# Two chained cross-attention layers: scores ahead of maxima in the fuller slots, V placed by ScalarE's queue, all splits of the prologue on GpSimd

## The chip, the core and the metric

The kernel runs on one core of one Trainium2 chip. The metric is the device time of one execution in microseconds (us). Before the change three runs took 943.01, 943.53 and 947.35 us; the median is 943.53 us.

The engines are named as in the profile: PE is TensorE's matrix multiplication and PEld its loading of weights, DVE is VectorE, ACT ScalarE, POOL GpSimd, and SP is SyncE, which here only issues DMAs. SPq and ACTq are the instruction queues of SP and ACT where they issue DMAs.

## What is computed

Two cross-attention layers follow one another over 32 sequences of 256 rows and 320 channels, with 20 heads of 16 channels, and 77 rows of context (512 channels). Cut to what matters, with the reference's other branches (which see no rows here) left out:

```python
for layer in (0, 1):                       # x: (32, 256, 320), ctx: (32, 77, 512)
    q = heads(x @ Wq)                      # 20 heads of 16 channels
    k, v = heads(ctx @ Wk), heads(ctx @ Wv)
    p = softmax(q @ k.T / sqrt(16))        # 256 x 77 for each head
    x = merge(p @ v) @ Wo + b + x
```

All of it is float32.

## The kernel before, in words

**Units.** Two sequences in one layer make a unit; there are 32 units. `units_in_order` (L86) takes the first layer four pairs ahead of the second, so that consecutive units do not depend on each other. Channels lie on partitions; a unit's 20 heads are five groups g of four tiles j, each tile two heads.

**Steps of a unit.** `keys` and `keys_rest` (L318, L336) project the context (`psk`), ACT copies it out (`kR`), and `mask_keys` writes two masked copies `kT`, on POOL but for the first unit (L274). `queries` and, for most units, `outputs_and_queries` (L358, L388) project x (`psq`), and ACT copies to `q`. `split_queries` (L297) divides q into a high and a low part that add up to it (`halves`, two buffers, three pieces of columns: L278 casts, L279 subtracts); `spread_queries` (L307) has SP issue four DMAs for each piece that lay the parts out anew (`qs`). `split_keys` and `spread_keys` do this to the keys (`kS`).

`maxima` (L491) multiplies q by kT (`psm`, L500) into four PSUM banks, and DVE takes maxima over the keys (`m`, L512). When all of a unit's are there, `turn` (L522) has DVE split and transpose them (L532 to L535, some 1.7 us) and SP issue four DMAs (L537) to `max_rows`. `scores` (L545) computes scores less maxima (`pss`: L550 with `max_rows`, L558 with `qs` and `kS`) into four PSUM banks, and ACT takes exponentials (`pT`, L564). `vals` (L428; `vals_of_few` for the last, short chunk) projects V for a chunk of 128 context rows (`psv`), ACT copies it to a `stage` (L442), and `place_vals` (L466) has a queue issue DMAs that put the rows of one unit into its tile `v`, mostly three for a unit (L485), and four more for the short chunk of each layer (L480). `values` (L607) multiplies pT by v (`po`, L578); DVE transposes (L590) and takes reciprocals (L594), POOL multiplies (L599), `turn_back` (L610) transposes once more on DVE to `oT` (L613). `finish` or `outputs_and_queries` projects it (`psy`), and `add` (L616) adds bias and x on DVE.

**Banks.** All products share eight PSUM banks that go round (`bank`, L108). A product begins when the bank that it takes has been read by the engine that empties it. In a slot with maxima and scores, the product behind them, the first `po`, takes the first bank of the eight: that of whichever of the two came first.

**Slots.** The order of the work is written out by hand. `at` (L656) puts a step under a slot number and a kind; L799 goes through the slots and emits the kinds of each in one fixed order: load, maxima, turn back, scores, values, rest, back, turn, split, full, last. Each engine runs its own instructions in this order. Slots below 1 are the prologue (L760 to L787). In steady state four units take 17 slots. The text names four kinds:

- A full slot (F) holds `outputs_and_queries`, mostly two `scores` and no `maxima`.
- Slot A behind it holds maxima, one `scores`, two `values`, `keys_rest`, the first half of a chunk's `vals`, `place_vals` of the older chunk, and in about half of the units `turn`.
- Slot B holds maxima, one `scores`, one `values`, one `keys`, the second half of `vals` and `place_vals` of the new chunk.
- Slot C holds maxima, one `scores`, one `values` and one `keys`.

Every DMA also waits for the completion of one that was issued about eight DMAs before it, on whichever queue that one is.

Of the kernel before, what the change touches and what calls it, by code (L numbers as in the profile page):

```python
# [58 lines left out]
B, S, C, CA, L = 32, 256, 320, 512, 77  # L59
# [36 lines left out]
def xattn_kernel(ctx: ExitStack, tc: tile.TileContext, xT, cT, cP, weights, outT):  # L96
    nc = tc.nc
# [46 lines left out]
    first, _, _ = PARTS["q"]  # L144
# [152 lines left out]
    def split_queries(u, i):  # L297

        a, b = PIECES[i]
        x = st[u]["halves", i] = work.tile(  # L300
            [P, 2, NT], F32R, tag="halves", name=f"halves_{u}_{i}", bufs=2
        )
        split(
            nc.gpsimd if u else nc.vector, x[:, 0, : b - a], x[:, 1, : b - a], st[u]["q"][:, a:b]
        )

    def spread_queries(u, i):  # L307
# [10 lines left out]
    def keys(u, t):  # L318
        p, layer = units[u]
        w, c_sb = w_sb[layer], cs[u]  # L320
        if t == 0:
            st[u]["kr"] = work.tile([P, NG, L], F32, tag="kR", name=f"kR_{u}", bufs=2)
        kR = st[u]["kr"]
        ps = bank(f"psk_{u}_{t}")
        for kc in range(NKA):
            by_columns(
                ps[:, 0 : 2 * L],
                w["k"][:, kc, t * P : (t + 1) * P],
                c_sb[:, kc, :],
                start=(kc == 0),  # L330
                stop=(kc == NKA - 1),
            )
        nc.scalar.copy(kR[:, 2 * t : 2 * t + 2].rearrange("p g k -> p (g k)"), ps[:, 0 : 2 * L])  # L333
        mask_keys(u, t)

    def keys_rest(u):  # L336

        p, layer = units[u]
        w, c_sb = w_sb[layer], cs[u]
        ps = bank(f"psk_{u}_2")  # L340
        for kc in range(NKA):
            for i in range(4):
                b, m = 1 - i // 2, i % 2
                nc.tensor.matmul(  # L344
                    ps[32 * i : 32 * i + 32, 0:L],
                    w["k"][:, kc, 2 * P + 32 * m : 2 * P + 32 * m + 32],
                    c_sb[:, kc, b * L : (b + 1) * L],
                    start=(kc == 0),
                    stop=(kc == NKA - 1),
                )  # L350
        nc.scalar.copy(st[u]["kr"][:, 4], ps[:, 0:L])
        mask_keys(u, 2)
# [5 lines left out]
    def queries(u):  # L358

        p, layer = units[u]  # L360
        w = w_sb[layer]
        q0 = new_queries(u)
        ps = [[bank(f"psq_{u}_{t}_{b}") for b in range(NB)] for t in range(2)]
        if u == 0:

            main_channels(ps, w["q"], xs[p], start=True, stop=False)
            last_channels(ps, w["q2"], xs[p], start=False, stop=True)
        else:
            rest = bank(f"psq_{u}_2")
            last_channels(ps, w["q2"], xs[p], start=True, stop=False)  # L370
            for b in range(NB):
                rest_last(rest, w["q22"], xs[p], b, swap=1, start=True, stop=False)
            rest_main(rest, w["q"], xs[p], start=False, stop=True, swap=1)
            nc.scalar.copy(of_group(q0, 4), rest[:, 0:S])
            main_channels(ps, w["q"], xs[p], start=False, stop=True)
        for g in range(4):
            nc.scalar.copy(of_group(q0, g), ps[g // 2][g % 2][:, 0:S])
# [88 lines left out]
    def place_vals(u, i):  # L466

        p, layer = units[u]
        if "v" not in st[u]:
            st[u]["v"] = work.tile(  # L470
                [P, NB, HEADS // 2, 2, 2, HD], F32, tag="v", name=f"v_{u}", bufs=2
            )
        for b in range(NB):
            first = (p * NB + b) * L
            k0, k1 = max(first, i * P), min(first + L, (i + 1) * P)
            if k0 < k1 and i in few:

                for m, a, r0, r1 in ((0, 0, 0, 3), (1, 0, 3, 6), (2, 0, 6, 9), (3, 2, 9, 10)):
                    o = 32 * m - i * P
                    nc.sync.dma_start(  # L480
                        out=st[u]["v"][k0 - first : k1 - first, b, r0:r1],
                        in_=stages[layer][i % 2][k0 + o : k1 + o, a : a + r1 - r0],
                    )
            elif k0 < k1:
                nc.sync.dma_start(  # L485
                    out=st[u]["v"][k0 - first : k1 - first, b],
                    in_=stages[layer][i % 2][k0 - i * P : k1 - i * P],
                )
# [118 lines left out]
    def values(u, g):  # L607
        st[u]["n", g] = divide(u, g, products(u, g))
# [44 lines left out]

    place = {}

    def at(slot, where, step):  # L656
        place.setdefault((slot, where), []).append(step)

    def start(u):

# [18 lines left out]
    for u, (p, layer) in enumerate(units):  # L679

        s = start(u - 2)
        if layer == 0 and u > 0:
            at(s - 5 - (u == 1), "load", lambda p=p: load_x(p))
        if u > 0:
            at(s - 4, "load", lambda u=u: load_context(u))
        if u > 1:
            k = (0, 1, 2) if u == 2 else (s - 2, s - 1, s + 1)
            at(k[0], "rest", lambda u=u: keys(u, 0))
            at(k[1], "rest", lambda u=u: keys(u, 1))
            at(k[2], "rest", lambda u=u: keys_rest(u))  # L690
        paired = u > 2 and u - 3 not in late
        if paired:
            at(s, "full", lambda u=u: outputs_and_queries(u - 3, u))
        elif u > 1:
            at(s, "last", lambda u=u: queries(u))
        if u > 1:
            at(s + 2, "split", lambda u=u: split_keys(u))
            at(start(u - 1), "load", lambda u=u: spread_keys(u))
            for i in range(3):
                at(start(u - 1) + i - 1, "split", lambda u=u, i=i: split_queries(u, i))  # L700
                at(start(u - 1) + i, "load", lambda u=u, i=i: spread_queries(u, i))
        need = range(p * NB * L // P, ((p + 1) * NB * L - 1) // P + 1)
        new = [i for i in need if i >= made[layer]]
        made[layer] += len(new)
        first = (-6, -2)[u] if u < 2 else start(u - 1) + 1
        slots = {}
        for k, i in enumerate(new):
            at(first - 3 - (u == 0) + k, "load", lambda layer=layer, i=i: load_chunk(layer, i))
            if i in few:
                slots[i] = first  # L710
                at(first, "full", lambda layer=layer, i=i: vals_of_few(layer, i))
                continue
            for h in range(2):
                slots[i] = first + (0 if u < 2 else k if len(new) > 1 else h)
                at(slots[i], "full", lambda layer=layer, i=i, h=h: vals(layer, i, h))
        for i in need:
            at(slots.get(i, first), "full", lambda u=u, i=i: place_vals(u, i))
        for g in range(NG):
            slot = slot_of(u, g)
            at(slot, "scores", lambda u=u, g=g: scores(u, g))  # L720
            at(slot + 1, "values", lambda u=u, g=g: values(u, g))
            if g < 4:
                at(slot + 2, "turn back", lambda u=u, g=g: turn_back(u, g))
            else:
                at(slot + 1, "back", lambda u=u, g=g: turn_back(u, g))
        if u == NU - 1:
            at(end, "full", lambda u=u: finish(u))
            at(end, "last", lambda u=u: finish_rest(u))
        if u in late:
            for t in range(2):  # L730
                at(late[u][t], "full", lambda u=u, t=t: finish(u, (t,)))
            at(late[u][2], "rest", lambda u=u: finish_rest(u))
            at(max(late[u]), "last", lambda u=u: store(u))


# [30 lines left out]
    at(-7, "split", lambda: split_keys(0))  # L766
    at(-6, "load", lambda: spread_keys(0))
    for i in range(3):
        at(-6 + i, "split", lambda i=i: split_queries(0, i))
        at(-5 + i, "load", lambda i=i: spread_queries(0, i))  # L770
    for slot, h, n in ((-6, 0, 3), (-6, 3, 3), (-4, 6, 2), (-4, 8, 2)):
        at(slot, "maxima", lambda h=h, n=n: maxima((0, h, n)))
    at(-4, "turn", lambda: turn(0))
# [1 line left out]
    at(-3, "split", lambda: split_keys(1))  # L775
    at(-2, "load", lambda: spread_keys(1))
    for i in range(3):
        at(-3 + i, "split", lambda i=i: split_queries(1, i))
        at(-2 + i, "load", lambda i=i: spread_queries(1, i))
    for slot, h, n in ((-2, 0, 3), (-2, 3, 2), (0, 5, 3)):  # L780
        at(slot, "maxima", lambda h=h, n=n: maxima((1, h, n)))
    at(1, "maxima", lambda: maxima((1, 8, 2), (2, 0, 1)))
# [2 lines left out]
    for u, slot in ((1, 1), (2, 4)):  # L785
# [7 lines left out]
    at(3, "load", lambda: load_weights(1, "v", "v", nc.sync))  # L793
    at(4, "load", lambda: load_weights(1, "o", "b", nc.sync))

    order = (
        "load", "maxima", "turn back", "scores", "values", "rest", "back", "turn", "split", "full", "last",
    )
    for slot in range(min(s for s, _ in place), max(s for s, _ in place) + 1):  # L799
        for where in order:  # L800
            for step in place.get((slot, where), ()):
                step()
# [98 lines left out]
```

## Time and profile before

| | |
|---|---|
| median of three runs | 943.53 us |
| profiled execution, its own time | 947.08 us |
| span of that execution, first to last instruction | 945.3 us, so 1.8 us lie around it |
| mean granted TensorE clock | 0.998 |
| share of the chain that ended last: PE, DVE, DMA, SPq | 88%, 7%, 2%, 1% |
| PE busy in the first 70 us | 63.0 us |
| PE busy from 60 us on (885.3 us) | 873.5 us |

The profile is one execution, taken by the hardware profiler. A group of instructions shows its busy time, the mean duration of one, the idle time of its engine just before it, and behind an arrow the instruction whose end released it. A row of the timeline starts with its start and its duration in us. Matmuls are pipelined and their ends are modelled, so that a busy PE is not PE at its peak; one float32 matmul appears as two records.

### The profile page before, as it was taken

To read this page: it belongs to the slowest core of one execution; us is meant where nothing else is said; L and a number is where in the kernel's file an instruction comes from. 1 tells how busy PE (TensorE), PEld (TensorE's weight loads), DVE (VectorE), ACT (ScalarE), POOL (GpSimd) and SP (SyncE) were. 2 spreads that over 40 slices of the span, in tenths; PEclk is the share of its full clock that TensorE was granted. 3 is DMA by queue.
4 is the path that set the end of the run, shared out by engine and by line. 5 is a ranking of instruction groups with operands and counts; after the bars stand their busy time and mean duration, and the time that the engine had idled before them with its cause. 6 is when DMAs were issued, how large, how long until landed. Compare 5 with 4: busy or idle time off the path is not lost.

```text
span 945.3 us, 48848 instructions
## 1 busy us (share of the span) xinstructions
PE 926.6 (98%) x21582; PEld 640.8 (68%) x21582; DVE 574.5 (61%) x1330; ACT 432.0 (46%) x975; POOL 406.9 (43%) x608
## 2 busy tenths in 40 slices
PE   8999999999999999999999999999999999999998
PEld 6666667766667666666766677666767666676654
DVE  4475557655577565665656666665566654776575
ACT  2254443644435534355443545335454354444462
POOL 2354445434455434455234454344553335543431
PEclk9999999999999999999999999999999999999999
DMA  6664444253453525536245352355433543353342
GB/s 227 196 217 129 133 147 145 82 172 120 163 153 95 197 76 163 165 104 201 68 145 176 98 201 82 125 175 161 153 96 120 160 155 119 92 162 105 118 136 97
DMA packets 114740, 133.03 MB, mean 141 GB/s; under 512 B 47012, under 2 KB 76004, under 8 KB 114530
## 3 DMA queue, kind: packets, MB, share of 16 engines
q1 hardware_dynamic: 113666, 127.42, 42.8%
q8 instruction: 170, 2.79, 1.3%
q10 hardware_dynamic: 864, 2.49, 0.7%
q14 instruction: 40, 0.33, 0.1%
HBM read 35.39 MB, written 10.49 MB: 49 GB/s over the span
## 4 chain that ended last, share of the span: by engine, by line
PE 88%; DVE 7%; DMA 2%; SPq 1%; issue 1%; POOL 0%; ACT 0%; POOLq 0%
PE psy L203 15%; PE po L578 15%; PE psq L203 14%; PE psm L500 10%; PE psv L203 7%; PE pss L558 7%; PE psk L203 7%; PE psy L237 4%; PE pss L550 4%; PE psq L237 3%; DVE m L512 3%; DVE turned L590 1%; PE psk L344 1%; DVE maxes L533 1%; SPq L316 1%; DMA x<-in_xT_dram 1%
## 5 line engine op out<-in xcount | busy, mean ns | idle before, releaser
L564 ACT ACTIVATE pT<-pss 77x512 f32<-77x512 f32 x640 | 324.4, 593 | 171.7 <-PE pss L558 171.0
L512 DVE TENSOR_REDUCE m<-psm 128x6 f32<-128x462 f32 (+2 forms) x512 | 248.3, 551 | 221.4 <-PE psm L500 220.9
L599 POOL TENSOR_TENSOR normal<-turned,inv 128x256 f32<-128x256 f32 x160 | 99.3, 621 | 484.5 <-DVE inv L594 457.5
L578 PE MATMUL po<-pT,v 77*32 77x256 f32 x2560 | 166.8, 385 | 8.3 <-DVE m L512 5.2
L203 PE MATMUL psy<-oT,w 128*32 128x256 f32 (+1 forms) x3072 | 164.5, 379 | 0.0
L203 PE MATMUL psq<-x,w 128*32 128x256 f32 (+1 forms) x3072 | 153.4, 380 | 0.6 <-DMA w<-in_w_dram 0.6
L203 PEld LDWEIGHTS psy<-oT,w 128*32 128x32 f32 (+1 forms) x3072 | 88.4, 108 | 63.4 <-issue 15.2
L590 DVE STREAM_TRANSPOSE turned<-po 128x512 f32<-128x512 f32 x160 | 109.5, 684 | 24.4 <-PE po L578 24.3
L203 PEld LDWEIGHTS psq<-x,w 128*32 128x32 f32 (+1 forms) x3072 | 86.8, 109 | 54.9 <-issue 2.2
L274 POOL TENSOR_SCALAR kT<-kR,masks 128x154 f32<-128x154 f32 x186 | 113.3, 619 | 19.2 <-ACT kR L333 19.2
L578 PEld LDWEIGHTS po<-pT,v 77*32 77x32 f32 x2560 | 72.4, 109 | 69.6 <-DVE m L512 26.7
L500 PE MATMUL psm<-kT,q 32*128 32x154 f32 x2560 | 116.2, 306 | 2.3 <-POOL kT L274 2.0
L500 PEld LDWEIGHTS psm<-kT,q 32*128 32x128 f32 x2560 | 90.1, 183 | 35.3 <-issue 25.3
L279 POOL TENSOR_TENSOR halves<-q,halves 128x512 fp32r<-128x512 f32 (+1 forms) x93 | 102.1, 1098 | 7.8
L558 PE MATMUL pss<-qs,kS 32*77 32x256 f32 x2560 | 104.6, 276 | 0.0
L620 DVE SCALAR_TENSOR_TENSOR x<-psy,w,x 128x256 f32<-128x256 f32 x160 | 68.3, 476 | 50.6 <-PE psy L203 49.2
L558 PEld LDWEIGHTS pss<-qs,kS 32*77 32x77 f32 x2560 | 89.2, 141 | 11.3
L613 DVE STREAM_TRANSPOSE oT<-normal 128x256 f32<-128x256 f32 x160 | 67.0, 431 | 45.8 <-POOL normal L599 45.8
L203 PE MATMUL psv<-w,cv 128*32 128x160 f32 x2432 | 93.5, 299 | 0.2 <-DVE m L512 0.2
L418 ACT COPY q<-psq 128x256 f32<-128x256 f32 x28 | 10.4, 372 | 161.8 <-PE psq L237 161.8
L203 PEld LDWEIGHTS psv<-w,cv 128*32 128x32 f32 x2432 | 77.8, 110 | 4.4 <-DVE m L512 0.6
L550 PE MATMUL pss<-max_rows,less 32*77 32x512 f32 x640 | 78.7, 468 | 1.4 <-DMA max_rows<-mT 1.4
(48 smaller groups left out, 725.3 us busy)
## 6 DMA issues: line engine op xcount, KB each, us to landing
qs<-halves SPq DMA_DIRECT2D x256, 128.0 KB
kS<-k_halves SPq DMA_DIRECT2D x128, 192.5 KB
c<-in_cP_dram SPq DMA_DIRECT2D x32, 308.0 KB
cv<-in_cT_dram SPq DMA_DIRECT2D x38, 256.0 KB
out_dram<-x SPq DMA_DIRECT2D x15, 640.0 KB
x<-in_xT_dram SPq DMA_DIRECT2D x14, 640.0 KB
qs<-halves SPq DMA_DIRECT2D x128, 64.0 KB
v<-stage SPq DMA_DIRECT2D x26, 192.5 KB
```

What stands on the lines that cost most here:

```text
L203: nc.tensor.matmul(out[m : m + 32], lhsT[:, m : m + 32], rhs, **flags)
L274: engine.tensor_scalar_mul(kT[:, e], kR[:, groups], masks[:, e : e + 1])
L279: engine.tensor_tensor(low, x, high.bitcast(F32), ALU.subtract)
L500: nc.tensor.matmul(ps[j][:, i * 2 * L : (i + 1) * 2 * L], q[r, c * P : (c + 1) * P], kT[r, :, g % 2, :], start=True, stop=True,)
L512: nc.vector.tensor_reduce(st[u]["m"].rearrange("p e h j -> p h e j")[:, first : first + n, :, j], ps[j][:, at * 2 * L : (at + n) * 2 * L]. ...
L550: nc.tensor.matmul(ps[j][:L], less[r, g % 4, :], max_rows[u % 2][r, g // 4], start=True, stop=False)
L558: nc.tensor.matmul(ps[j][:L, e * S : (e + 1) * S], st[u]["ks"][r, e, g, half, :], q[r, :], start=False, stop=(half == 1 and e == 1),)
L564: nc.scalar.activation(st[u]["p", g][j][:L], ps[j][:L], AF.Exp, scale=SCALE)
L578: nc.tensor.matmul(po[o : o + 32, e * S : (e + 1) * S], vpad[:L, b, pair, e].rearrange("p a d -> p (a d)"), pT[j][:L, e * S : (e + 1) * S] ...
L590: nc.vector.transpose(turned[:, 0 : 2 * S], po)
L599: nc.gpsimd.tensor_tensor(normal.rearrange("p q e d -> p e q d"), outs, inv.unsqueeze(3).broadcast_to([P, 2, S // 32, HD]), ALU.mult,)
L620: nc.vector.scalar_tensor_tensor(x, ps[:, 0:S], w_sb[layer]["b"][:, 0, t : t + 1], x, ALU.add, ALU.add)
```

## The change

There are three edits.

1. Steps under `at` carry a count of PE columns (`work_of`). In a slot above 0 whose count is over 10 * S = 2560, the kinds are emitted as load, scores, turn back, maxima; in all other slots as before. By these counts all slots F, A and B come under the new order (A has 3944, 5224 or 4200, B 3536 to 4816), while C (2256), slots of 2304 and the prologue keep the old one. 60 slots have both scores and maxima and the new order.
2. `place_vals` issues its DMAs from ACT's queue instead of SP's: 100 at L485 and 8 at L480.
3. In the prologue `split_queries` of unit 0 goes from DVE to POOL, and the splits and their `spread_queries` stand in earlier slots: pieces 0 and 1 together, right behind the queries, piece 2 one slot later. For unit 1, pieces 0 and 1 come together too, and piece 2 goes to slot 0, behind that slot's `keys`. `split_keys` of unit 0 stays on DVE.

```diff
@@ split_queries
-            nc.gpsimd if u else nc.vector, x[:, 0, : b - a], x[:, 1, : b - a], st[u]["q"][:, a:b]
+            nc.gpsimd, x[:, 0, : b - a], x[:, 1, : b - a], st[u]["q"][:, a:b]
@@ place_vals, in both places
-                nc.sync.dma_start(
+                nc.scalar.dma_start(
@@ at
-    def at(slot, where, step):
+    work_of = {}
+
+    def at(slot, where, step, columns=0):
+
         place.setdefault((slot, where), []).append(step)
+        work_of[slot] = work_of.get(slot, 0) + columns
...
-            at(k[0], "rest", lambda u=u: keys(u, 0))
+            at(k[0], "rest", lambda u=u: keys(u, 0), 8 * 2 * L)
...
-            at(s, "full", lambda u=u: outputs_and_queries(u - 3, u))
+            at(s, "full", lambda u=u: outputs_and_queries(u - 3, u), 50 * S)
...
-                at(slots[i], "full", lambda layer=layer, i=i, h=h: vals(layer, i, h))
+                at(slots[i], "full", lambda layer=layer, i=i, h=h: vals(layer, i, h), 4 * C)
...
-            at(slot + 1, "values", lambda u=u, g=g: values(u, g))
+            at(slot + 1, "values", lambda u=u, g=g: values(u, g), 4 * S)
...
@@ the prologue, unit 0 and unit 1
-        at(-6 + i, "split", lambda i=i: split_queries(0, i))
-        at(-5 + i, "load", lambda i=i: spread_queries(0, i))
+        at(-7 + i // 2, "split", lambda i=i: split_queries(0, i))
+        at(-6 + i // 2, "load", lambda i=i: spread_queries(0, i))
...
-        at(-3 + i, "split", lambda i=i: split_queries(1, i))
-        at(-2 + i, "load", lambda i=i: spread_queries(1, i))
+        at(-3 + 3 * (i // 2), "split", lambda i=i: split_queries(1, i))
+        at(-2 + 3 * (i // 2), "load", lambda i=i: spread_queries(1, i))
@@ the loop over the slots
-    order = (
-        "load", "maxima", "turn back", "scores", "values", "rest", "back", "turn", "split", "full", "last",
-    )
+    rest = ("values", "rest", "back", "turn", "split", "full", "last")
     for slot in range(min(s for s, _ in place), max(s for s, _ in place) + 1):
+        if slot > 0 and work_of[slot] > 10 * S:
+            order = ("load", "scores", "turn back", "maxima") + rest
+        else:
+            order = ("load", "maxima", "turn back", "scores") + rest
```

## The prediction

> **What bounds the kernel.** I read the page first, then the waits by engine, then the timeline: the first 60 us, and one stretch of steady state (226 to 242 us).
>
> ```profile
> PE 926.6 (98%) x21582; PEld 640.8 (68%) x21582; DVE 574.5 (61%) x1330; ACT 432.0 (46%) x975; POOL 406.9 (43%) x608
> L578 PE MATMUL po<-pT,v 77*32 77x256 f32 x2560 | 166.8, 385 | 8.3 <-DVE m L512 5.2
> ```
>
> PE is the bound, and no edit takes a product away. A gain can only come from PE's pauses, 18.7 us in all. The waits say whose they are (total, times, longest):
>
> ```profile
> PEld po L578 <- DVE m L512: 26.7, 89, 1.1
> PE po L578 <- DVE m L512: 5.2, 11, 0.9
> PE psm L500 <- POOL kT L274: 2.0, 1, 2.0
> PE pss L550 <- DMA max_rows<-mT: 1.4, 1, 1.4
> ```
>
> The 26.7 us of PEld are no prize: 89 waits of 0.3 each, and in slot F, where no maxima stand, po's weights also wait 0.28 (at 186.24, named ACT pT). That is the end of the product before. What can be had is 5.2 us in 11 places, and the prologue.
>
> **The prologue.**
>
> ```profile
> 29.05 4.62 SPq L316 DMA_DIRECT2D qs<-halves  x4
> ...
> 34.41 2.71 SPq L537 DMA_DIRECT2D max_rows<-mT  x4
> ...
> 39.95 0.46 PE L550 MATMUL pss<-max_rows,less 32*77 32x512 f32 x4 [1.44 <-DMA max_rows<-mT]
> ...
> 48.17 0.40 POOL L278 CAST halves<-q 128x256 fp32r<-128x256 f32 x1 [4.70 <-DMA qs<-halves]
> ...
> 49.35 1.34 POOL L274 TENSOR_SCALAR kT<-kR,masks 128x154 f32<-128x154 f32 x2
> 50.75 0.55 PE L500 MATMUL psm<-kT,q 32*128 32x154 f32 x8 [2.05 <-POOL kT L274]
> ...
> 52.33 1.94 PE L578 MATMUL po<-pT,v 77*32 77x256 f32 x16
> ```
>
> Two queues are held by pieces of q. SP: mT is ready at 27.95, but its DMAs stand behind those of q's pieces and go out only at 34.41. POOL: unit 2's kT stands behind unit 1's third piece, which waits 4.70 for a buffer; PE then waits 2.05 and comes back at a lower clock (granted 0.50 in 52 to 54 us).
>
> After the change, step by step:
> - Unit 0's splits leave DVE (0.42 + 0.69 twice). Its second reduces start 0.5 earlier, and `psk` at 24.00, which waits for one of them, gains 0.5.
> - POOL splits pieces 0 and 1 (0.61 + 1.28 each, from the steady rows) by about 15 us. SP sends kS at 15.26 to 18.97, then eight qs (0.6 each) to 23.8, two loads, the third piece to 27.4, two loads, and mT at 28.6 instead of 34.41; it lands near 34. L550 then waits only for PE: 2.3 earlier in all.
> - `kT` of unit 2 stands ahead of the third split of unit 1, so the 2.05 goes: 2.3 + 2.05 and the split first part of psm make 4.6 at the second L550.
> - With no pause the clock stays: po costs 0.88 instead of 1.71 to its successor, psk 1.17 instead of 1.53. 6.1 by slot 2.
> - What is late next: DVE. Its 2.54 of reduces, 0.95 of L590 and L594 and 1.7 of `turn` now end 1.3 after PE wants po of slot 2; before, that wait was 0.25. 1.1 comes back.
>
> Sum: **5.0** gained (from 2.3, if kT's wait only changes its name, to 6.1). Three v DMAs on ACT ahead of the first exponentials hold these by about 1; `psq` wants their banks later than that.
>
> **Scores ahead of maxima.**
>
> ```profile
> 231.65 0.29 ACT L442 COPY stage<-psv 128x160 f32<-128x160 f32 x1 [0.86 <-PE psv L203]
> ...
> 232.71 0.45 DVE L535 STREAM_TRANSPOSE mT<-maxes 128x256 f32<-128x256 f32 x1
> ...
> 233.08 2.24 DVE L512 TENSOR_REDUCE m<-psm 128x6 f32<-128x462 f32 x4
> ...
> 233.38 2.04 ACT L564 ACTIVATE pT<-pss 77x512 f32<-77x512 f32 x4 [1.44 <-PE pss L558]
> ...
> 233.74 1.07 PE L578 MATMUL po<-pT,v 77*32 77x256 f32 x16 [0.45 <-DVE m L512]
> ```
>
> This is slot B behind an A with `turn`. The turn keeps DVE to 233.16, the reduce starts late, and po waits 0.45 for its first bank. In the new order po takes the bank of the first exponential: L550 to exponential takes 1.1 (232.31 to 233.38), the exponential 0.59, in all 1.69; L550 to po takes 1.79 (0.72 of scores, 0.84 and 0.25 of maxima, as now in the other order). Slack 0.1. Of the eleven waits nine of 0.44 to 0.46 stand in such slots: **4.1** gained. (The 0.25 of 57.61 is in the prologue, and the 0.90 of 810.68 in a slot that keeps the old order.)
>
> Late next is DVE in slot C. Maxima now end 0.71 later in A, and DVE has no pause from there: 233.08 + 0.71, two L613 (0.67), four reduces (2.16), L590 and L594 (0.96), first reduce of C (0.63) end at 238.21, where C's po wants its bank at 238.66 - 0.45 = 238.21. A knife edge: between 0 and 0.45 each, I take 0.1: **-0.9** (0 to -4.1).
>
> The trace shows no pss ahead of psm and no psm ahead of po. Changes of weights beside them cost 0.16 (psm to psv, 17.68) to 0.42 (35.05); psv to psm 0.25, psv to pss 0.24, pss to po 0.26. Nearest is 0.26, so the 60 slots change by nothing; 0.1 either way would be 6.
>
> **V from ACT's queue.** SP loses 108 issues, but nothing on PE waits for SP in steady state: gain 0. ACT gets them in order, between `stage` copy and the next exponentials.
>
> ```profile
> L120 SPq DMA_DIRECT2D x<-in_xT_dram x14: 347/587/621, 24.2 to 740.8; - x14
> L120 ACTq DMA_DIRECT2D x<-in_xT_dram x1: 334/334/334, 4.8 to 4.8; - x1
> L485 SPq DMA_DIRECT2D v<-stage x100: 593/807/1647, 20.5 to 917.8; - x100
> ```
>
> (Durations: shortest/median/longest.) ACT shows none of this form. One x load took 334 ns on ACT and 587 on SP; v took 807 on SP. Bounds are 0.33 and 0.81; I take 807 x 334/587 = 0.46. An ACT instruction behind a DMA waits for its issue: the table load starts at 7.37, the DMA of 7.00 took 0.34.
>
> B's exponential is due 1.1 after L550, with 0.1 of slack; ACT can issue from 0.13 after L550 (old chunk) or 0.43 (fresh). Slots A with one DMA lose nothing. Seven with two of the old chunk free ACT at 0.13 + 0.92: nothing. One with two fresh ones: 0.15. Six with three, at 0.13 + 1.38 against 1.2: 0.31 each, 1.9. Near the end six DMAs, four of them shorter (L480, 588 ns on SP), hold the exponentials of 912.71 by 1.3. Sum **-3.3** (-0.7 at 0.33, -15.8 at 0.81). B's DMAs stand ahead of C's exponentials, and C's po waits for DVE: nothing, but for a wait on mT's DMAs, which may hold ACT for up to 1.
>
> The Trainium skill, "DMA: Bandwidth & Descriptors" (Issuing engines are not separate DMA queues), says that issuing from several engines saves only sequencer time. It speaks against this edit: SP has that time to spare, ACT pays it. Taken alone it makes the edit a loss.
>
> The skill's "TensorE: Matmul & The Clock Gate" (Part 1) lets the clock fall after an idle window of about 3.4 us. Here a recorded idle of 2.05 went before the 0.50, so the trace differs; by the rule the 1.2 of clock would not return, and the prologue would give an estimated 3.8.
>
> **Sum.** 5.0 + 4.1 - 0.9 - 3.3 = 4.9 off the profiled 947.08: 942.2. That execution was 3.55 above the median of 943.53, so **938.6**.
>
> **Rivals.**
> - *Slower: ACT pays as SP did.* At 0.81 ACT loses 15.8: 5.0 + 4.1 - 0.9 - 15.8 = -7.6, **951.1**. For: L485 never went under 593 on SP. Against: ACT's five early issues took 0.33 to 0.47. It decides from about 0.6 an issue, where ACT eats the 8.2 of the rest.
> - *The wait moves to C:* all 4.1 come back: 1.7, **941.8**. For: DVE's chain has no gap. Against: the arithmetic ends level.
> - *The prologue gives half:* 2.3 instead of 5.0: 2.2, **941.3**. For: SP's queue is in order, and loads stand between the pieces.
> - *All goes well:* ACT at 0.33, no wait in C, 6.1 in the prologue: 6.1 + 4.1 - 0.7 = 9.5, **934.0**.
>
> **Chances.** Forecast 0.30, ACT slow 0.18, wait moves 0.20, prologue halved 0.08, all well 0.24. What a measurement can tell from no change is 0.5%, 4.7 us: 938.8 to 948.2. The forecast lies by its edge; I count 0.18 of it below and 0.12 within. Faster 0.18 + 0.24 = 0.42, same 0.12 + 0.20 + 0.08 = 0.40, slower 0.18. Range 932.5 to 949.5: it takes in the good case with 1.5 for the unseen changes of weights, and the lower half of the slow case, and leaves out about 0.15. The likeliest case alone spans 936 to 941.
>
> **What would show it.** Prologue: the second L550 near 46 instead of 51, no granted clock under 1 at 50 to 55, po of slot 2 waiting over 1 for DVE. Steady state: no `PE po <- DVE m` in B; a new one in C refutes the knife edge; `PE po <- ACT pT` in B behind three DMAs shows ACT's price. I am wrong if L485 on ACT is over 0.6, or if slots in the new order are longer where nothing waits.

## The result and the profile after

The changed kernel takes 991.56 us (median of four runs, 987.96 to 996.11) against 944.53 for the kernel before: ratio 1.0497, 95% interval 1.0446 to 1.0548. The forecast was 938.6, its range 932.5 to 949.5; it was wrong, in sign too.

The profiled execution took 987.96 with a span of 986.2, which is 40.9 more than before. First its line of busy times and the group of po, as the page shows them:

```profile
PE 941.3 (95%) x21582; PEld 642.7 (65%) x21582; DVE 574.5 (58%) x1324; ACT 433.0 (44%) x975; POOL 413.1 (42%) x614
...
L578 PE MATMUL po<-pT,v 77*32 77x256 f32 x2560 | 168.3, 388 | 30.4 <-ACT pT L564 27.4
```

PE does the same 21582 records and is busy 14.7 longer; its idle time goes from 18.7 to 44.9. The wait ahead of po was DVE's; now it is ACT's. The waits by engine (total, times, longest):

```profile
ACT pT L564 <- DMA v<-stage: 45.6, 12, 11.1
...
PE po L578 <- ACT pT L564: 27.4, 16, 8.9
...
PE pss L550 <- DMA max_rows<-mT: 3.4, 2, 2.8
...
PE po L578 <- DVE m L512: 2.5, 2, 1.5
```

The nine waits of 0.45 are gone (the two left are in the prologue and in a slot with the old order). But ACT, for which PE waited nowhere before, now holds its exponentials behind its own V DMAs. By the starts of the 28 F slots:

| stretch | before | after | longer by |
|---|---|---|---|
| start to the first F slot | 69.49 | 72.72 | 3.2 |
| first to 28th F slot | 778.10 | 800.41 | 22.3 |
| 28th F slot to the end | 97.71 | 113.04 | 15.3 |

Two kinds of wait make this up. The first is occupation. The group of L485 and a slot B of the timeline (start, duration):

```profile
L485 ACTq DMA_DIRECT2D v<-stage x100: 553/760/1436, 23.0 to 945.1; - x100
```

```profile
176.94 0.29 ACT L442 COPY stage<-psv 128x160 f32<-128x160 f32 x1 [0.79 <-PE psv L203]
176.95 2.39 ACTq L485 DMA_DIRECT2D v<-stage  x3
...
179.39 2.04 ACT L564 ACTIVATE pT<-pss 77x512 f32<-77x512 f32 x4 [2.15 <-DMA v<-stage]
...
180.03 1.07 PE L578 MATMUL po<-pT,v 77*32 77x256 f32 x16 [1.50 <-ACT pT L564]
```

Three issues of 0.76 in a row keep ACT from the exponentials for 2.15, and po, which in the new order takes the bank of the first of them, waits 1.50. The second kind is a wait inside ACT's queue. The timeline around the A slot at 676:

```profile
669.07 10.96 SPq L316 DMA_DIRECT2D qs<-halves  x8
...
676.13 4.53 ACTq L485 DMA_DIRECT2D v<-stage  x3
...
677.05 0.40 POOL L278 CAST halves<-q 128x256 fp32r<-128x256 f32 x1
...
680.70 2.04 ACT L564 ACTIVATE pT<-pss 77x512 f32<-77x512 f32 x4 [4.36 <-DMA qs<-halves]
...
681.35 1.55 PE L578 MATMUL po<-pT,v 77*32 77x256 f32 x16 [3.72 <-ACT pT L564]
```

Every DMA waits on the semaphore that it raises itself, and eight of these go round both queues. The third V DMA starts at 679.99; the last DMA on its semaphore was one of SP for the third piece of q, which had to wait for POOL's split, went out at 677.47 and landed at 679.97. ACT runs in order, so the exponentials stood behind it. A V DMA that starts within 0.11 us of the landing that it waits for is called held below. In this trace 24 of 108 are held: 12 behind one of mT's (L537), 11 behind a piece of q (L316), one behind V itself. At the end the same happens to all exponentials of one slot:

```profile
942.23 6.06 SPq L316 DMA_DIRECT2D qs<-halves  x8
942.81 3.04 ACTq L485 DMA_DIRECT2D v<-stage  x2
947.10 2.92 ACTq L480 DMA_DIRECT2D v<-stage  x4
950.07 1.56 ACT L564 ACTIVATE pT<-pss 77x512 f32<-77x512 f32 x3 [9.48 <-DMA v<-stage]
950.71 3.64 PE L578 MATMUL po<-pT,v 77*32 77x256 f32 x32 [8.86 <-ACT pT L564]
```

The 32 records of po take 3.64 here and 1.93 at 671.34. The lower clock is where more than half of the 14.7 of busy time come from: the granted clock is 0.50 for 3.4 us beside the pauses at 39, 47, 681 and 835 each, and for 13.7 from 944.6. PE is busy for 21.0 of these 27.3 us, since the last stretch begins inside the long pause; in the kernel before it is 3.4 of 3.4. Half the difference, 8.8, is an estimate of what the clock added.

### The profile page after: what moved, and what is told of

Read it like the earlier page. It is cut to its first block, busy times and chain, and to the rows that moved or that the text cites. A ratio compares the mean times of both kernels' runs of the same rounds, so it can differ in the third digit from the quotient of the medians.

```text
span 986.2 us, 48442 instructions
## 1 busy us (share of the span) xinstructions
PE 941.3 (95%) x21582; PEld 642.7 (65%) x21582; DVE 574.5 (58%) x1324; ACT 433.0 (44%) x975; POOL 413.1 (42%) x614
## 4 chain that ended last, share of the span: by engine, by line
PE 73%; DVE 10%; DMA 4%; issue 4%; POOL 3%; SPq 2%; ACTq 2%; ACT 2%; POOLq 0%; DVEq 0%
PE psq L203 14%; PE psy L203 13%; PE po L578 12%; PE psm L500 6%; PE pss L558 6%; PE psv L203 5%; PE psk L203 5%; DVE m L512 4%; PE pss L550 4%; PE psy L237 4%; PE psq L237 4%; DMA qs<-halves 2%; DVE turned L590 2%; DVE maxes L533 1%; ACTq L485 1%
## 5 line engine op out<-in xcount | busy, mean ns | idle before, releaser
L203 PE MATMUL psq<-x,w 128*32 128x256 f32 (+1 forms) x3072 | 157.3, 382 | 3.8 <-ACT pT L564 3.5
L578 PEld LDWEIGHTS po<-pT,v 77*32 77x32 f32 x2560 | 70.1, 110 | 90.1 <-ACT pT L564 43.4
L500 PE MATMUL psm<-kT,q 32*128 32x154 f32 x2560 | 112.1, 298 | 0.0
L279 POOL TENSOR_TENSOR halves<-q,halves 128x512 fp32r<-128x512 f32 (+1 forms) x96 | 106.8, 1112 | 8.0
L558 PE MATMUL pss<-qs,kS 32*77 32x256 f32 x2560 | 108.0, 276 | 0.0
L500 PEld LDWEIGHTS psm<-kT,q 32*128 32x128 f32 x2560 | 92.6, 184 | 13.8 <-issue 10.2
L550 PE MATMUL pss<-max_rows,less 32*77 32x512 f32 x640 | 85.1, 454 | 5.7 <-DMA max_rows<-mT 3.4
L203 PE MATMUL psk<-c,w 128*32 128x154 f32 x2048 | 81.8, 301 | 0.0
```

Of the source, the lines that this page charges most:

```text
L203: nc.tensor.matmul(out[m : m + 32], lhsT[:, m : m + 32], rhs, **flags)
L279: engine.tensor_tensor(low, x, high.bitcast(F32), ALU.subtract)
L500: nc.tensor.matmul(ps[j][:, i * 2 * L : (i + 1) * 2 * L], q[r, c * P : (c + 1) * P], kT[r, :, g % 2, :], start=True, stop=True,)
L550: nc.tensor.matmul(ps[j][:L], less[r, g % 4, :], max_rows[u % 2][r, g // 4], start=True, stop=False)
L558: nc.tensor.matmul(ps[j][:L, e * S : (e + 1) * S], st[u]["ks"][r, e, g, half, :], q[r, :], start=False, stop=(half == 1 and e == 1),)
L578: nc.tensor.matmul(po[o : o + 32, e * S : (e + 1) * S], vpad[:L, b, pair, e].rearrange("p a d -> p (a d)"), pT[j][:L, e * S : (e + 1) * S] ...
```

## The experiments

**Theory A:** V's DMAs hold ACT, above all by their waits for landings. **B:** the new order itself is slow. **C:** prologue and tail make most of it. **D:** what costs is the time that each issue takes. Differences below are of medians; ratios are to the kernel before, with 95% intervals.

### One edit at a time

Each edit alone on the kernel before, and the changed kernel without the second:

```diff
 v_back_on_sp: the changed kernel, in place_vals
-                nc.scalar.dma_start(
+                nc.sync.dma_start(
 v_on_act_alone: the kernel before, in place_vals
-                nc.sync.dma_start(
+                nc.scalar.dma_start(
 order_alone: the kernel before with work_of and the choice of order
 prologue_alone: the kernel before with split_queries on nc.gpsimd in the new slots
```

> The changed kernel with V's DMAs back on SP's queue: the new order and the new prologue without the second edit. Theory A (ACT is held by V's DMAs: each waits in ACT's queue until a DMA some eight places earlier, most of them SP's, has landed; the exponentials queued behind it come late, and the first po of a slot in the new order takes the bank of the first exponential): the 27.4 us of `PE po <- ACT pT` and the 45.6 of `ACT pT <- DMA v` go, and the time comes to 938 to 944 us. Theory B (the new order itself is slow, ACT's waits are only where it shows): 965 to 990, and the waits of po stay under another name. Theory C (the prologue and the tail make most of it): 955 to 975, F slots level with those of before from the second on.

> The kernel before with the second edit alone: V's DMAs on ACT's queue, old order, old prologue. In the old order the first po takes a bank that DVE empties, and the banks of the scores are wanted only some four products later, so a late exponential has about 2 us more. Theory A: ACT still waits some 30 to 45 us behind V's DMAs, but little of it reaches PE in steady state (0 to 6 us); prologue and tail may pay up to 12: 945 to 960. If it is only the issue time of 0.76 us each, whatever the order: 944 to 950, and no wait of ACT on a DMA above 1 us. If the second edit costs its 48 by itself: 980 to 992.

> The kernel before with the first edit alone: scores ahead of maxima in slots above 2560 columns; V stays on SP, the prologue is the old one. Theory A: the nine waits of 0.45 go, slots C pay 0 to 4: 938 to 944. Theory B (the order is slow): above 955.

> The kernel before with the third edit alone: all splits of the prologue on GpSimd, in earlier slots. By the prediction the second L550 comes near 46 instead of 51 and the time falls by 2.3 to 6.1: 937.5 to 941. By the rival that the prologue itself lost (in the changed kernel the first F slot came 3.2 later): 945 to 948.

| kernel | us | ratio |
|---|---|---|
| v_back_on_sp | 942.98 | 0.9982 (0.9957 to 1.0007) |
| v_on_act_alone | 981.03 | 1.0381 (1.0351 to 1.0412) |
| order_alone | 943.05 | 0.9983 (0.9962 to 1.0003) |
| prologue_alone | 944.71 | 0.9999 (0.9986 to 1.0013) |

B and C fall: without the second edit nothing is lost, and order and prologue alone lose nothing. But A as I had put it falls too. I had expected 945 to 960 for V on ACT in the old order; it took 981.03, 36.0 more than before. Its waits:

```profile
ACT pT L564 <- DMA v<-stage: 47.3, 13, 9.9
...
PE po L578 <- ACT pT L564: 9.3, 1, 9.3
...
PE psq L203 <- ACT pT L564: 6.5, 1, 6.5
```

The slack of some 2 us in the old order hides short waits, and 20 of the 27 steps from F slot to F slot in this trace are within 0.3 of those of before. But seven are 0.9 to 3.7 longer, and prologue and tail take 3.0 and 13.7. The edit is dearer still in the new order: 991.56 - 942.98 = 48.6.

### Occupation without a wait

V stays on SP; where ACT issued its DMAs, it does a copy that waits for no DMA:

```diff
                 nc.sync.dma_start(
                     out=st[u]["v"][k0 - first : k1 - first, b],
...
                 )
+                nc.scalar.copy(junk, ones[:, 0:1].broadcast_to([P, 680]))
```

> The kernel before, with V's DMAs left on SP; in their place ACT does a copy of a constant into an unused tile, 128x680, some 0.7 us long, which waits for no DMA. It puts the occupation of 0.76 us an issue on ACT without any wait behind SP's DMAs, in the old order. Theory A (in the old order the 36 us come from waits for landings, not from the issues): the time stays near that of before, 944 to 948. Theory D (the time that an issue takes is what costs): 970 to 982.

> The same copies on ACT in the kernel that has the first edit alone (943.05 without them). Theory A': in the new order a slot B has little slack behind two or three issues, so the occupation alone shows as `PE po <- ACT pT` of 0.4 to 1.9 in some 14 slots: 954 to 959. If the new order has as much slack as the old one: 943 to 946. Theory D: 970 to 985.

dummy_old_order took 952.52 (1.0075, 1.0051 to 1.0099), dummy_new_order 958.81 (1.0148, 1.0123 to 1.0174). In dummy_new_order (its lines stand 3 lower: L567 and L581 are the exponentials and po) the copy, a slot B and a wait read:

```profile
L491 ACT CAST junk<-ones x100: 757/760/770, 20.5 to 920.2; 128x680 bf16<-128x680 f32 x100
```

```profile
171.45 2.34 ACT L491 CAST junk<-ones 128x680 bf16<-128x680 f32 x3
173.70 2.04 ACT L567 ACTIVATE pT<-pss 77x512 f32<-77x512 f32 x4
...
174.34 1.07 PE L581 MATMUL po<-pT,v 77*32 77x256 f32 x16 [1.48 <-ACT pT L567]
```

```profile
PE po L581 <- ACT pT L567: 18.5, 16, 3.9
```

The copy takes 760 ns, as an issue does, and gives the same wait in the same slot: 1.48 against 1.50. So the occupation costs 958.81 - 943.05 = 15.8 in the new order. In the old one it costs 8.5, more than A expected: the six copies of the last unit hold po for 3.9, and the tail of the profiled execution is 6.9 longer. Of its 27 steps from F slot to F slot only two are over 0.3 longer (0.4 and 1.4). Its prologue is 4.2 shorter than in the profile of before; why, I did not pursue. D falls: of the 48.6, 48.6 - 15.8 = 32.8 are something else than occupation.

### V later on ACT

```diff
-            at(slots.get(i, first), "full", lambda u=u, i=i: place_vals(u, i))
+            at(slots.get(i, first) + 1, "full", lambda u=u, i=i: place_vals(u, i))
```

> The kernel before with V's DMAs on ACT's queue (981.03 as it was), each place_vals one slot later; queue, count and issue time are the same. In the old places those that were held came some three us behind mT's DMAs or the third piece of q on SP. Theory A: a slot later these have landed, so in steady state the steps of 1.5 to 3.7 from F slot to F slot go, and the time falls by 8 to 17, to 964 to 973; prologue and tail may change either way by some 5. Theory D: 978 to 984, no change.

In this kernel a unit that needs two fresh chunks takes the rows of its oldest chunk from the chunk that has overwritten that stage; the amount of work is unchanged. It took 986.33 (1.0426, 1.0377 to 1.0474): no theory's number. Its trace has 17 held DMAs instead of 22: 4 behind mT's instead of 9, but 12 behind pieces of q instead of 10. The wait has moved, not gone. It tells nothing between the theories.

### The held DMAs alone

```diff
+    BACK = {(3, 4), (22, 11), (23, 16), (8, 3), (28, 15), ...}
     def place_vals(u, i):
         p, layer = units[u]
+        queue = nc.sync if (u, i) in BACK else nc.scalar
...
-                nc.scalar.dma_start(
+                queue.dma_start(
```

> The changed kernel (991.56), but the 19 calls of place_vals in which its trace shows a V DMA that started within 0.11 us of the landing that it waits for go back to SP: 34 of 108 DMAs. Theory A (waits for landings cost some 33 of the 48.6 that V on ACT costs in this order, the occupation by 108 issues some 16): the 33 go, and the last unit's occupation with them: 948 to 962, if few others come to be held instead. Theory D (every V DMA on ACT costs alike): 34/108 of 48.6, 15 less: 974 to 979.

> The counterpart: the changed kernel with 34 other V DMAs back on SP, in 24 calls of place_vals none of whose DMAs was held. Theory A: only some of the occupation goes, the waits stay: 983 to 991. Theory D: 974 to 979, as with the other 34.

> The old order and the old prologue with V on ACT (981.03), but the 19 calls of place_vals with held DMAs in that trace on SP, 35 of 108. Theory A: the 73 others cost nothing in the old order: 945 to 952. Theory D: 35/108 of 36.5, 12 less: 967 to 971.

| V on ACT | us | ratio | held |
|---|---|---|---|
| all 108 (changed kernel) | 991.56 | 1.0497 (1.0446 to 1.0548) | 24 |
| without 34, the held ones among them | 958.57 | 1.0145 (1.0112 to 1.0178) | 0 of 74 |
| without 34 others | 986.87 | 1.0434 (1.0405 to 1.0464) | 23 of 74 |
| old order, without 35, the held ones among them | 944.67 | 0.9998 (0.9983 to 1.0013) | 0 of 73 |

This settles it. The same number of DMAs moved is worth 33.0 or 4.7 (the intervals of the changed kernel and of the 34 others overlap). In the old order the 35 make all of the loss, and the other 73 cost nothing on ACT. What is left in held_on_sp is mostly the occupation (its po is L581):

```profile
PE po L581 <- ACT pT L567: 14.9, 15, 1.7
```

The 34 include the six DMAs of the last unit, whose occupation alone held po for 3.9 in dummy_new_order. Of the other waits of po for exponentials, 14.6 there, 14.9 stand here. So the waits for landings cost an estimated 29 of the 33.0.

### Versions that beat both

With V on SP a stall of another kind spreads the runs (937.96 to 948.63). In v_back_on_sp SP sends V behind mT, and ACT's next copy into that stage waits for its landing:

```profile
458.19 3.84 SPq L537 DMA_DIRECT2D max_rows<-mT  x4
...
462.46 2.46 SPq L485 DMA_DIRECT2D v<-stage  x3
...
466.49 0.49 ACT L442 COPY stage<-psv 128x160 f32<-128x160 f32 x2 [5.59 <-DMA v<-stage]
...
466.83 0.90 PE L550 MATMUL pss<-max_rows,less 32*77 32x512 f32 x2 [2.95 <-ACT stage L442]
```

```diff
 v_sp_before_turn: v_back_on_sp with
-            at(slots.get(i, first), "full", lambda u=u, i=i: place_vals(u, i))
+            at(slots.get(i, first), "full" if i in slots else "back", lambda u=u, i=i: place_vals(u, i))
 mt_ahead_of_piece: that, and in the prologue
-        at(-6 + i // 2, "load", lambda i=i: spread_queries(0, i))
+        at(-6 if i < 2 else -4, "load" if i < 2 else "full", lambda i=i: spread_queries(0, i))
```

> The new order and the new prologue with V on SP (942.98, 937.96 to 948.63 in ten runs), but the older chunk's place_vals stands ahead of the slot's turn, so that on SP V's DMAs do not stand behind mT's. In the profile of the version without this, ACT's copy into stage waits 5.6 us for such DMAs in one slot and PE loses 2.9 at 467. If that stall is what spreads the runs: 938 to 941 and a spread of under 4; if mT, now behind V, becomes late instead: 943 to 950.

> The version with V on SP ahead of the turn (940.12), and in the prologue SP issues the third piece of unit 0's q behind mT instead of ahead of it. It tests the step of the prediction that failed in the prologue: mT's DMAs at 28.6, where the run of the third edit alone shows 33.93, behind that piece, and a first L550 that waits 2.67 with a clock of 0.50 behind it. If the piece ahead of mT is what holds mT: mT goes out near 30, the wait of L550 and the slow clock go, and the first F slot comes 3 to 4.5 earlier: 935.5 to 938. If the landing waits of the loads ahead of it hold SP just as long: mT after 32.5, and 939 to 941.

v_sp_before_turn took 940.12 (0.9959, 0.9944 to 0.9975), 939.03 to 943.20: no copy into stage waits for V, and the spread falls from 10.7 to 4.2. mt_ahead_of_piece took 939.10 (0.9938, 0.9921 to 0.9956). Its SP and PE:

```profile
30.70 2.93 SPq L537 DMA_DIRECT2D max_rows<-mT  x4
```

```profile
38.28 0.46 PE L550 MATMUL pss<-max_rows,less 32*77 32x512 f32 x4 [2.44 <-DMA max_rows<-mT]
38.55 0.83 PE L558 MATMUL pss<-qs,kS 32*77 32x256 f32 x16
39.31 2.28 PE L203 MATMUL psk<-c,w 128*32 128x154 f32 x32
```

mT goes out near 30 as hoped, but L550 still waits 2.44 and the slow psk is still there. mT's four DMAs now take 5.1 to 5.8 to land, where they took 2.8 to 4.9 in v_sp_before_turn and 3.3 to 4.3 in the kernel before. From 30 to 34 us the share of the DMA engines reads 1.03, at 326 GB/s; in the kernel before, where mT is in flight from 34 on, it reads 0.80 from 34 to 38, at 200. Loads of cv, x, c and w, 1.7 MB, go out just ahead, from 27.53 on; that they slow the landing is likely, but no run shows it alone. SP sends mT 2.8 earlier than in v_sp_before_turn, and the last of the four lands 0.9 earlier: the landing took most of the gain back. The median is 1.0 under that of v_sp_before_turn, which the spreads (936.91 to 941.98 here) do not settle.

## Why the prediction was wrong, step by step

**V from ACT's queue, -3.3: the step that failed, at 48.6.** Two parts.
- *The price of an issue.* I took 807 x 334/587 = 0.46, scaling from a load of x; the chip took 0.76. With 0.76 the same slots give about 13.9 (six slots at 1.21, seven at 0.45, one at 0.75, and 2.8 at the end); the copies of this length cost 15.8. That the upper bound, 0.81, gave just 15.8 is chance. The trace of dummy_new_order has six waits of 1.48 to 1.49 and eight of 0.69 to 0.70 in these slots, so slots and mechanism were right, most waits came some 0.25 above the sum's, and the price was wrong: the row of the same form, 0.81 on SP, was nearer than a ratio taken from another form. The forecast's own bound, an issue over 0.6, was passed.
- *"Nothing, but for a wait on mT's DMAs, which may hold ACT for up to 1".* This is the term of 32.8. I knew that each DMA waits for one some eight before it, but put nothing for it into the sum: I named it only behind mT's DMAs, only ahead of slot C's exponentials, and at up to 1. On ACT 24 were held, 12 of them by mT's and 11 by pieces of q, and one pause reached 8.86. No rival held it; the slower one had only the price of an issue, and its 951.1 is 40 short.

The prediction cited the Trainium skill, "DMA: Bandwidth & Descriptors" (Issuing engines are not separate DMA queues), for the rule that issuing from several engines saves sequencer time only. The runs agree: with 73 of 108 V DMAs off SP and none of them held (held_on_sp_old_order), the time is that of before, 944.67 against 944.46. What ACT lost behind SP's landings, 32.8, the rule does not speak of.

**Scores ahead of maxima, 4.1 - 0.9 = 3.2: right by the profiles, too small to show in the whole time.** In order_alone the 27 steps from F slot to F slot are 4.5 shorter together and the nine waits of 0.45 are gone. Of the slots that keep the old order one has po waiting 1.51 for DVE, where before it was 0.90, and the others do not wait: 0.6 for the 0.9 that I gave back. In the whole time it is 2.0, within its interval; in v_sp_before_turn the same steps are 5.6 shorter. The price is that the slots grow sensitive: by the copies late exponentials cost 0.7 or 1.5 a slot in 14 slots of the new order, and in the old one they show in two steps only (0.4 and 1.4). The prediction's slack of 0.1 held this, but it charged it only to the price of an issue. (The 0.16 and 0.42 that it read as changes of weights are waits for DVE in their rows; the sum does not use them.)

**Prologue, 5.0: right in two of its parts, mis-sized in the third.** The prologue of prologue_alone, from its timeline:

```profile
18.81 6.70 SPq L316 DMA_DIRECT2D qs<-halves  x8
...
24.03 0.40 POOL L278 CAST halves<-q 128x256 fp32r<-128x256 f32 x1 [9.61 <-DMA qs<-halves]
...
25.61 2.66 SPq L485 DMA_DIRECT2D v<-stage  x3
...
30.25 2.45 SPq L316 DMA_DIRECT2D qs<-halves  x4
...
33.93 3.53 SPq L537 DMA_DIRECT2D max_rows<-mT  x4
...
39.54 0.46 PE L550 MATMUL pss<-max_rows,less 32*77 32x512 f32 x4 [2.67 <-DMA max_rows<-mT]
...
40.41 2.29 PE L203 MATMUL psk<-c,w 128*32 128x154 f32 x32
...
49.85 0.51 PE L550 MATMUL pss<-max_rows,less 32*77 32x512 f32 x4
...
50.96 1.07 PE L578 MATMUL po<-pT,v 77*32 77x256 f32 x16
...
55.82 1.07 PE L578 MATMUL po<-pT,v 77*32 77x256 f32 x16 [1.03 <-DVE m L512]
```

kT's wait of 2.05 is gone, the first po takes 1.07 instead of 1.94, and the next one waits 1.03 for DVE, where I had 1.1. But mT goes out at 33.93, not 28.6: eight qs took 6.70 instead of 4.8, the third split waited 9.61 for its buffer, and V's three DMAs stood between. (The forecast had V on ACT; there mT goes out at 33.65.) So L550 waits 2.67, the clock falls behind it, and the second L550 comes at 49.85, not 46. The first F slot gains 1.8, not 5.0, and not even that is sure: with the old prologue it comes 1.4 earlier than before in order_alone and 4.2 in dummy_old_order. In the whole time the edit brings 0.3 (945.04 - 944.71), well within its interval. In the changed kernel ACT's holds turn this into a loss: ACT is idle for 6.08 ahead of a copy of kR and for 11.10 ahead of the first exponentials, psq waits 3.46 for these, and the first F slot comes 3.2 later than before. (The steps that the prediction lists for the prologue come to 5.8 of its 6.1.)

**The clock.** The prediction weighed the Trainium skill, "TensorE: Matmul & The Clock Gate" (Part 1), an idle window of about 3.4 us, against a fall after 2.05. These runs side with the row: in held_on_sp a granted clock of 0.50 for 3.4 us follows waits of 1.66 (at 378) and 1.44 (at 903); other waits of this length had none. What decides between them can be read from the traces: within each of the 14 the granted clock changes only on a grid of 3.413 us. Of the grid's stretches at a clock of 1.00, all 31 in which PE is busy for under 0.50 of the time are followed by a clock of 0.50, 9 of the 35 with 0.50 to 0.62, 1 of the 35 with 0.62 to 0.75, and none of the 3735 above. So it matters how a pause lies on the grid: the one at 378 leaves PE busy for 0.51 of the stretch from 375.4, and the clock falls; the 1.50 of the changed kernel's slot B leaves 0.56 of that from 176.6, and it does not.

**Sum.** The two edits that I gave 8.2 bring 2.1 in v_back_on_sp (945.04 - 942.98), within its interval, and 3.9 once V's order on SP is mended (944.04 - 940.12). The third, at -3.3, brought -48.6.

## What to carry to other kernels

Before a DMA moves to the queue of an engine that computes, look up what its instruction waits for: an engine in order passes each such wait on to all that stands behind it, however idle it is on average. Take the price of an issue from the same form, on whichever queue it is seen. And a reorder that removes slack is priced with the other edits in place: the same occupation cost 8.5 in one order and 15.8 in the other.

## What the hardware showed that I had not expected

- An issue's time goes by the form of the transfer: on ACT 0.33 for a load of x, 0.76 (median of 100) for V; on SP 0.59 and 0.81.
- Pauses of 1.44 to 2.05 us were followed, though not always, by 3.4 us at a clock of 0.50, and the long pause near the end of the changed kernel by 13.7: in these traces it goes by PE's busy share of a stretch on a grid of 3.413 us, with the turn at about one half.
